# Re-planning an adaLN feed-forward block on one core: new duration tables, smaller transfer margins for the last pair, four PSUM banks for the quarter that TensorE turns

## The chip, the cores and the metric

The kernel runs on one core of one Trainium2 chip. The metric is the device time of that core in microseconds. A run of the kernel before took 563.19 us (median of 3 runs, 563.15 to 563.2).

## The reference

Two conditioning rows select shift, scale and gate by a matmul (adaLN); `x` is 2 x 2048 tokens of 512 features, all in float32.

```
emb = silu(t) @ ada_w + ada_b            # 6 groups of 512
shift_msa, scale_msa, gate_msa, shift_mlp, scale_mlp, gate_mlp = split(emb, 6)
norm = ln(x) * (1 + scale_msa) + shift_msa
h = gelu(norm @ ssm_w1 + ssm_b1);  x = x + gate_msa * (h @ ssm_w2 + ssm_b2)
norm2 = ln(x) * (1 + scale_mlp) + shift_mlp
hf = gelu(norm2 @ ff_w1 + ff_b1)         # 512 -> 1024
x = x + gate_mlp * (hf @ ff_w2 + ff_b2)  # 1024 -> 512
```

## The kernel before

**The work.** The 4096 tokens are eight blocks of 512. Each block is normalized, modulated, turned (features on partitions) and passed through `ssm1` and `ssm2`; then the feed-forward pair follows for four pairs of blocks, `ff1 0`, `ff2 0`, ..., `ff1 3`, `ff2 3`. The four matrix products are done by the Strassen-Winograd scheme, seven products of half-size blocks in place of eight, and in `ff1` and `ff2` the scheme is used twice. TensorE (PE) therefore has fewer matmuls, and VectorE (DVE) and GpSimd (POOL) have hundreds of adds instead: sums of operand blocks that matmuls read, and sums that take products out of PSUM banks. A product lands in one of eight banks, and the next product for that bank waits until the adds have read the last one.

**What sets the order.** Nothing runs when the code calls it. Each helper (`tt` for adds at L258, `act`, `copy`, `mm` at L296, `turn_by_pe` at L306, `dma` at L318) records an operation with a cost, a latency and its dependencies in `Plan`. The PE operations keep the order of the code. `Plan.order` works back from the PE operations to a due time for every other operation; `Plan.simulate` then plays the engines forward, and on each takes the most urgent of the operations that could start by its reckoning. An add whose operands lie in SBUF may go to DVE or POOL, whichever reaches it first. The resulting order is what each engine's queue holds, and on the chip a queue runs strictly in that order: an instruction that waits holds all behind it. Costs and latencies are written into the helpers as numbers. DMAs are reckoned with a `care` that stretches them, so that the operations ahead of them are due earlier.

**The start.** PE does nine 512-wide matmuls and one transpose of 48 rows of conditioning data into bank 1 (L306); DVE copies them out (`cols`, L1318). Meanwhile DVE computes mean and variance of the first four token tiles (`BN_STATS` L526, `BN_AGGR` L527; tiles 0 and 1 in `marks_128`, 2 and 3 in `marks_129`), POOL takes the power -0.5 (L559, L560), DVE refines it (L562 to L565) and scales tile 0 (L585), ACT scales tile 1 (L276). PE then makes `modulation` 0 and 1 (L296, 128x128), turns tiles 0 and 1 by eight transposes between the two halves of modulation 1, and tiles 2 and 3 by eight behind it; DVE and ACT take them out (L660, L276), and `ssm1` begins.

**The end.** Of the output of the last pair (`ff2 3`), quarters are turned back by a DVE transpose (L1073, in `quarter_out`) and a trip through DRAM (`back<-far`, then `rows<-back`), and added to the residual (`far<-rows`, `near<-rows`, L258), which is sent out. The last quarter is turned by PE instead (`turned_by_pe`): two transposes of 128x128 per piece into a PSUM bank, a DVE add of that bank to the residual (`hidden<-bank`, 128x2x128), and a DMA of 128 KB. `TURNED_AT` gives the bank: for block 0 of the pair 3 and 4, for block 1 of the pair 2 and 0, one bank for each half, so the two pieces of a half (`e` 0 and 1) share it. `L1049` is the scaled add that takes a finished product out of PSUM into `rows`.

In the listings of orders and in the profile, `rows`, `hidden`, `near`, `far`, `turned`, `ring`, `fw` are SBUF regions; `bank_72` to `bank_79` are PSUM banks 0 to 7.

Of the kernel before, what the change touches and what calls it, by code (L numbers as in the profile page):

```python
# [12 lines left out]
ALU = mybir.AluOpType  # L13
# [7 lines left out]
class Plan:  # L21
# [8 lines left out]
    ISSUE, FLIGHT, LANDING, RATE, BACKLOG = 640.0, 1300.0, 700.0, 370.0, 4000.0  # L30
    NEAR, SPARE = 30000.0, 1500.0
    RATED, LANDED = 0.5, 4000.0
    LITTLE = 1 << 15
    LANES = 8
    AHEAD, SLACK = 2500.0, 150.0

# [76 lines left out]
    def simulate(self):  # L113
        ops, hop = self.ops, self.HOP
        left, ready = [len(op.deps) for op in ops], [0.0] * len(ops)
        free = dict.fromkeys("pvags", 0.0)
        self.lock, pipe, holder = 0.0, 0.0, None
        tensor = [op for op in ops if op.engs == "p"]
        at, pools, found = 0, {e: [] for e in "vags"}, {}
        lanes = [0.0] * self.LANES  # L120

        def enter(op):
            if op.lead and op.late < 1e8:
                ready[op.n] = max(ready[op.n], op.late - op.lead)
            for e in op.engs:
                if e != "p":
                    pools[e].append(op)
                    found.pop(e, None)

        def choose(e):  # L130
            pool = pools[e]
            if not pool:
                return None
            at = {}
            for op in pool:
                backlog = self.BACKLOG if op.late < free[e] + self.NEAR else self.SPARE
                wait = self.lock if e in op.shared else pipe - backlog if op.size > self.LITTLE else 0.0
                at[op.n] = max(free[e], ready[op.n], wait, lanes[0] if op.size else 0.0)
            now = min(at.values())

            def rank(op):
                return op.late + (self.AHEAD if e == "v" and len(op.engs) > 1 else 0.0), op.n

            op = min((op for op in pool if at[op.n] <= now), key=rank)
            end = now + op.cost[e]
            soon = [u for u in pool if now < at[u.n] < end - self.SLACK and u.late < min(end, op.late)]
            if soon:
                op = min(soon, key=lambda u: (at[u.n], u.n))
            return at[op.n], op

        for op in ops:
            if not op.deps:
                enter(op)
        count = len(ops)
        while count:
            best = None
            if at < len(tensor) and not left[tensor[at].n]:
                best = (max(free["p"], ready[tensor[at].n]), -1.0, "p", tensor[at])
            for e in "avgs":
                if e not in found:  # L160
                    found[e] = choose(e)
                c = found[e]
                if c and (best is None or (c[0], c[1].late) < best[:2]):
                    best = (c[0], c[1].late, e, c[1])
            start, _, e, op = best
            op.on, op.start, op.after = e, start, None
            free_at, free[e] = free[e], start + op.cost[e]
            if op.size > self.LITTLE:
                pipe = max(start + self.FLIGHT, pipe) + op.size / self.RATE * (1 + self.RATED * op.care)
                op.end = pipe + self.LANDING + self.LANDED * op.care  # L170
                found.pop("a", None), found.pop("s", None)
            else:
                op.end = start + op.lat[e]
                if op.size and e == "s":
                    op.end = max(op.end, pipe + self.LANDING)
            if op.size:
                lanes = lanes[1:] + [op.end]
                found.pop("a", None), found.pop("s", None)
            if e in op.shared:
                if e == "g" and holder and holder.on == "v" and start > max(free_at, ready[op.n]):  # L180
                    op.after = holder
                self.lock, holder = start + op.cost[e], op
                found.clear()
            if e == "p":
                at += 1
            else:
                for x in op.engs:
                    pools[x].remove(op)
                    found.pop(x, None)
            count -= 1  # L190
            for s in op.succ:
                o = ops[s]
                gap = 0.0 if o.engs == e and not op.size else hop
                ready[s] = max(ready[s], op.end + gap)
                left[s] -= 1
                if not left[s] and o.engs != "p":
                    enter(o)
# [3 lines left out]
def kernel(  # L201
# [62 lines left out]
        )  # L264

    def small(e, fn, o, ins, cost=None):
        cost = cost or {"v": 110, "g": 210}[e]
        plan.add(e, fn, [o], ins, {e: cost}, {e: cost + 75}, "g")

    def act(o, a, func, bias=0.0, scale=1.0):  # L270
        n = cols(o)
        ptrs = [p for p in (bias, scale) if not isinstance(p, float)]
        cost = n / 1.4 + (155, 215, 340)[len(ptrs)] + (30 if func == AF.Gelu_apprx_tanh else 0)
        plan.add(
            "a",
            lambda E: E.activation(o, a, func, bias=bias, scale=scale),  # L276
            [o],
            [a] + ptrs,
            {"a": cost},
            {"a": cost + 90},  # L280
        )

    def copy(o, a):
        cost = cols(o) / 1.4 + 150
        plan.add("a", lambda E: E.copy(o, a), [o], [a], {"a": cost}, {"a": cost + 60})  # L285

    def mm(o, lhsT, rhs, start, stop, at=None):
        n = cols(rhs)
        if at is None:
            cost = {128: 223.0, 256: 431.6, 512: 853.0}.get(n, 2 * (n / 1.2 + 3))  # L290
            kw = {}
        else:
            cost, kw = 68.0, {"tile_position": at}
        plan.add(
            "p",
            lambda E: E.matmul(o, lhsT, rhs, start=start, stop=stop, skip_group_check=True, **kw),  # L296
            [o],
            [lhsT, rhs],
            {"p": cost},
            {"p": cost + 165},  # L300
        )
# [218 lines left out]
    def stats(xt, slots=range(C)):  # L520
        t = marks[norms[0] % 4]
        norms[0] += 1
        mv = cut(t[:, :8], "p (c two) -> p c two", c=C)
        for c in slots:
            st, src, dst = t[:, 8 + 6 * c : 14 + 6 * c], xt[:, c, :], mv[:, c, :]
            plan.add("v", lambda E, st=st, src=src: E.bn_stats(st, src), [st], [src], {"v": 694}, {"v": 680})  # L526
            plan.add("v", lambda E, st=st, dst=dst: E.bn_aggr(dst, st), [dst], [st], {"v": 100}, {"v": 182})  # L527
        return t, mv

    STATS_BY_ACT = (4, 5)  # L530

    def act_sum(o, a, func, total, bias, scale):
        ptrs = [] if isinstance(bias, float) else [bias]
        cost = cols(o) / 1.4 + (440, 540)[len(ptrs)]
        plan.add(
            "a",
            lambda E: E.activation(o, a, func, bias=bias, scale=scale, accum_out=total),
            [o, total],
            [a] + ptrs,
            {"a": cost},  # L540
            {"a": cost + 90},
        )
# [12 lines left out]
    def scales(t, mv, v="g", slots=slice(0, C)):  # L555
# [1 line left out]
        ve, r, e, rstd, nmr = [a[:, slots] for a in full]  # L557
        var, mean, half = mv[:, slots, 1], mv[:, slots, 0], half_t[:, slots]
        small("g", lambda E: E.tensor_scalar(ve, var, 1.0, EPS, ALU.mult, ALU.add), ve, [var])  # L559
        small("g", lambda E: E.tensor_tensor(r, ve, half, ALU.pow), r, [ve, half], 1090)  # L560
        if v == "v":
            small(v, lambda E: E.tensor_tensor(e, r, ve, ALU.mult), e, [r, ve])  # L562
            small(v, lambda E: E.scalar_tensor_tensor(e, e, -0.5, r, ALU.mult, ALU.mult), e, [e, r])
# [28 lines left out]
    def turn(bl, src, c):  # L592
        o = cut(bl, "p (m k c q) -> p k m c q", m=C, k=KD, c=C)[:, :, :, c, :]
        a = cut(slot(src, c), "p (k m q) -> p k m q", k=KD, m=C)
        plan.add("v", lambda E: E.transpose(o, a), [o], [a], {"v": 636}, {"v": 705})

    def modulate(t, k, which, b):
        o = t[:, :, k * P : (k + 1) * P]
# [466 lines left out]
    def quarter_out(s, d, blk, r, scaled=False):  # L1065
# [4 lines left out]
        band = cut(bands[n], "p (a c e r) -> p e c a r", a=M, c=C, e=2)  # L1070
        for e in range(2):
            o, a = band[:, e], cut(done[:, e], "p (c a q) -> p c a q", c=C, a=M)
            plan.add("v", lambda E, o=o, a=a: E.transpose(o, a), [o], [a], {"v": 636}, {"v": 705})  # L1073
        closing = s + 1 == NBLK // 2
        queue = lambda f: "sa"[f % 2] if closing else "s"
        far_t = back_d[s][d][blk]
        for f in range(M):
# [16 lines left out]
        if not closing:  # L1094
            dma(to, x)
        quarters[0] += 1

    def down(s):
        q = {f"{o + 1}{blk + 1}": hC[:, blk, :, 2 * o : 2 * o + 2, :] for o in range(2) for blk in range(2)}
# [81 lines left out]

        return sums, last_sum, prepare, leaf

    TURNED_AT = ((3, 4), (2, 0))
    tail, waiting, leaves_read = [{}, {}], [], [0]

    def turned_by_pe(blk, r, f, quad):
# [3 lines left out]

        def turned_back():
            e, h = int(quad[0]) - 1, int(quad[1]) - 1
            bank = cut(banks[TURNED_AT[blk][h]], "p (c e d) -> p c e d", c=2, e=2)
            for c in range(2):
                col = slice((2 * h + c) * P, (2 * h + c + 1) * P)
                turn_by_pe(bank[:, c, e], summed[:, r, e, col], ident, c == 0 and h not in got, c == 1)
            got[h] = True
            c, d = slice(2 * h, 2 * h + 2), slice(e * P, (e + 1) * P)
            x = got["x"][:, c, d]  # L1200
# [250 lines left out]
```

## Time and profile before

| | |
|---|---|
| median of the runs | 563.19 us |
| profiled execution, its time | 563.11 us |
| span of its trace | 561.3 us |
| mean granted TensorE clock | 0.998 |
| PE busy | 552.9 us (98%), 2809 matmul records |
| DVE busy | 479.2 us (85%), 848 instructions |
| POOL busy | 385.0 us (69%), 475 |
| ACT busy | 282.9 us (50%), 523 |
| DMA | 123.68 MB, mean 220 GB/s |

The profiled execution's own time is 1.8 us above the span, which runs from the first to the last record. PE records overlap, so where time is lost on PE is read from the distance between starts: a 128x256 record begins 0.216 us after the one before it when nothing holds it, a group of four 0.86 us after the last four.

### The profile page before, as it was taken

What the parts mean: (1) busy time and instruction counts of PE and PEld (TensorE: products, weight loads), DVE (VectorE), ACT (ScalarE), POOL (GpSimd) and SP (SyncE); (2) the same over time, 40 slices, a digit from 0 to 9 for tenths busy, and PEclk for the clock granted to TensorE, in tenths of its full rate; (3) what the DMA queues carried; (4) which work ended last, traced back from release to release, by engine and by line L of the source; (5) the groups of instructions that cost most, each with busy time, mean ns of one, the idle gap of its engine ahead of it and who ended that gap; (6) DMA issues with size and microseconds to landing.
All of it is one profiled execution on the core that took longest, in us unless ns stands there. A gap on an engine that the chain in (4) does not pass through costs nothing.

```text
span 561.3 us, 8747 instructions
## 1 busy us (share of the span) xinstructions
PE 552.9 (98%) x2809; PEld 481.7 (86%) x2809; DVE 479.2 (85%) x848; ACT 282.9 (50%) x523; POOL 385.0 (69%) x475
## 2 busy tenths in 40 slices
PE   8999999999999999999999999999999999999995
PEld 4888889888898988888888888888888888888884
DVE  5696888888779578899999997789988989998987
ACT  3473866674877844666205347414247414244230
POOL 2887747979946299985646868676767766547581
PEclk9999999999999999999999999999999999999999
DMA  8963799988399978995201999611998612983417
GB/s 313 398 229 82 233 363 309 316 259 269 106 276 327 291 311 249 330 292 171 57 20 38 286 322 301 226 39 45 303 325 286 212 39 67 312 288 122 140 45 218
DMA packets 66945, 123.68 MB, mean 220 GB/s; under 512 B 5668, under 2 KB 34260, under 8 KB 65364
## 3 DMA queue, kind: packets, MB, share of 16 engines
q1 hardware_dynamic: 64080, 121.27, 65.9%
q10 hardware_dynamic: 2820, 1.86, 1.3%
q8 instruction: 22, 0.36, 0.3%
q14 instruction: 23, 0.19, 0.1%
HBM read 77.89 MB, written 44.18 MB: 217 GB/s over the span
## 4 chain that ended last, share of the span: by engine, by line
PE 91%; DVE 6%; DMA 2%; POOL 0%; issue 0%; DVEq 0%; POOLq 0%
PE bank L296 90%; DVE rows L258 2%; DVE near L258 1%; DMA fw<-in_L_cond_ada_w_dram 1%; DVE far L258 1%; PE bank L306 1%; DVE fw L258 1%; DVE hidden L258 0%; DMA fw<-in_L_cond_ada_b_dram 0%; DVE far L1073 0%; POOL far L258 0%; POOL fw L258 0%; POOL rows L258 0%; DVE turned L660 0%; DVE rows L1049 0%
## 5 line engine op out<-in xcount | busy, mean ns | idle before, releaser
L296 PE MATMUL bank<-turned,ring 128*128 128x256 f32 x896 | 210.2, 380 | 0.2 <-DVE turned L660 0.2
L296 PEld LDWEIGHTS bank<-turned,ring 128*128 128x128 f32 x896 | 168.0, 190 | 23.1 <-DVE turned L660 0.4
L258 DVE TENSOR_TENSOR hidden<-bank,hidden 128x512 f32<-128x512 f32 (+2 forms) x178 | 126.4, 738 | 23.9 <-PE bank L296 19.9
L296 PE MATMUL bank<-near,hidden 128*128 128x256 f32 (+1 forms) x470 | 95.1, 350 | 0.0
L296 PEld LDWEIGHTS bank<-near,hidden 128*128 128x128 f32 x470 | 82.2, 191 | 9.3 <-POOL near L258 0.3
L296 PE MATMUL bank<-far,fw 128*128 128x256 f32 (+1 forms) x354 | 86.0, 374 | 0.2
L258 POOL TENSOR_TENSOR turned<-turned 128x512 f32<-128x512 f32 (+1 forms) x62 | 70.4, 1148 | 20.4 <-DVE turned L258 9.0
L296 PE MATMUL bank<-ring 128*128 128x256 f32 x336 | 82.4, 380 | 0.0
L258 DVE TENSOR_TENSOR rows<-bank,rows 128x256 f32<-128x256 f32 (+1 forms) x142 | 66.1, 478 | 16.0 <-PE bank L296 11.9
L296 PEld LDWEIGHTS bank<-far,fw 128*128 128x128 f32 x354 | 66.5, 190 | 9.6 <-issue 0.5
L296 PEld LDWEIGHTS bank<-ring 128*128 128x128 f32 x336 | 63.7, 190 | 9.0 <-issue 0.5
L285 ACT COPY bank<-bank 128x512 f32<-128x512 f32 (+2 forms) x84 | 37.7, 449 | 63.0 <-PE bank L296 62.2
L276 ACT ACTIVATE hidden<-hidden,cols 128x512 f32<-128x512 f32 (+1 forms) x66 | 44.7, 710 | 42.9 <-DVE hidden L258 42.9
L258 POOL TENSOR_TENSOR hidden<-hidden 128x128 f32<-128x128 f32 (+2 forms) x45 | 43.5, 976 | 25.3 <-DVE hidden L258 13.1
L296 PE MATMUL bank<-near,fw 128*128 128x256 f32 (+1 forms) x246 | 60.7, 377 | 0.0
L296 PE MATMUL bank<-hidden,fw 128*128 128x256 f32 (+1 forms) x216 | 53.3, 376 | 0.4 <-DVE rows L258 0.4
L296 PEld LDWEIGHTS bank<-near,fw 128*128 128x128 f32 x246 | 46.1, 190 | 6.4 <-issue 0.2
L276 ACT ACTIVATE turned<-turned,mod,mod 128x512 f32<-128x512 f32 x56 | 42.2, 807 | 9.0 <-DMA turned<-turned 8.4
L296 PEld LDWEIGHTS bank<-hidden,fw 128*128 128x128 f32 x216 | 40.3, 190 | 6.5 <-DVE rows L258 0.8
L258 POOL TENSOR_TENSOR ring<-turned,ring 128x256 f32<-128x256 f32 x42 | 30.6, 740 | 20.7 <-PE bank L296 17.0
L276 ACT ACTIVATE rows<-rows,gb,mod 128x512 f32<-128x512 f32 (+1 forms) x34 | 26.5, 787 | 34.9 <-DVE rows L258 25.0
L258 POOL TENSOR_TENSOR fw<-fw 128x256 f32<-128x256 f32 (+1 forms) x38 | 35.6, 944 | 11.8 <-DMA fw_parts<-fw 4.3
(123 smaller groups left out, 735.7 us busy)
## 6 DMA issues: line engine op xcount, KB each, us to landing
ring<-fw_parts SPq DMA_DIRECT2D x28, 512.0 KB, 4.8
turned<-far SPq DMA_DIRECT2D x52, 256.0 KB, 4.2
ring<-fw_parts SPq DMA_DIRECT2D x28, 384.0 KB, 5.2
turned<-turned SPq DMA_DIRECT2D x32, 256.0 KB, 5.4
back<-far SPq DMA_DIRECT2D x52, 128.0 KB, 2.9
rows<-back SPq DMA_DIRECT2D x13, 512.0 KB, 5.1
fw_parts<-fw SPq DMA_DIRECT2D x21, 256.0 KB, 4.6
fw<-in_L_cond_ada_w_dram SPq DMA_DIRECT2D x5, 1024.0 KB
```

Source lines behind the costliest of these rows:

```text
L258: lambda E: E.tensor_tensor(o, a, b, f),
L276: lambda E: E.activation(o, a, func, bias=bias, scale=scale),
L285: plan.add("a", lambda E: E.copy(o, a), [o], [a], {"a": cost}, {"a": cost + 60})
L296: lambda E: E.matmul(o, lhsT, rhs, start=start, stop=stop, skip_group_check=True, **kw),
L306: lambda E: E.matmul(o, a, identity, start=start, stop=stop, is_transpose=True, skip_group_check=True),
```

## The change

It changes numbers, and one table. In `Plan` the engines start at 700 ns instead of 0, and large DMAs at 2650. The cost and latency of several kinds of operations are replaced: small POOL and DVE operations, narrow ACT operations, copies, accumulating ACT operations, the modulation matmuls, `BN_STATS` (694 to 585), `BN_AGGR`, the power, the DVE transposes. In `quarter_out` the DMAs of the last pair are recorded with `care` 0.1. `TURNED_AT` gets a bank for every piece, so that block 0 uses banks 3, 0, 2 and 4 for its four pieces.

```diff
-    LITTLE = 1 << 15
+    LITTLE, FIRST = 1 << 15, 2650.0
...
-        free = dict.fromkeys("pvags", 0.0)
-        self.lock, pipe, holder = 0.0, 0.0, None
+        free = dict.fromkeys("pvags", 700.0)
+        self.lock, pipe, holder = 0.0, self.FIRST, None
...
-            plan.add("v", lambda E, st=st, src=src: E.bn_stats(st, src), [st], [src], {"v": 694}, {"v": 680})
-            plan.add("v", lambda E, st=st, dst=dst: E.bn_aggr(dst, st), [dst], [st], {"v": 100}, {"v": 182})
+            plan.add("v", lambda E, st=st, src=src: E.bn_stats(st, src), [st], [src], {"v": 585}, {"v": 680})
+            plan.add("v", lambda E, st=st, dst=dst: E.bn_aggr(dst, st), [dst], [st], {"v": 90}, {"v": 178})
...
         closing = s + 1 == NBLK // 2
+        care, plan.care = plan.care, 0.1 if closing else plan.care
...
         quarters[0] += 1
+        plan.care = care
...
-    TURNED_AT = ((3, 4), (2, 0))
+    TURNED_AT = (((3, 0), (2, 4)), ((2, 2), (0, 0)))
...
-            bank = cut(banks[TURNED_AT[blk][h]], "p (c e d) -> p c e d", c=2, e=2)
+            bank = cut(banks[TURNED_AT[blk][h][e]], "p (c e d) -> p c e d", c=2, e=2)
...
-                turn_by_pe(bank[:, c, e], summed[:, r, e, col], ident, c == 0 and h not in got, c == 1)
+                turn_by_pe(bank[:, c, e], summed[:, r, e, col], ident, c == 0 and (not blk or h not in got), c == 1)
```

PE's order stays the same up to the last six transposes. On DVE and POOL nearly the whole queue is permuted: 93 adds that DVE did are POOL's now, and 88 of POOL's are DVE's (DVE 848 instructions before and 845 now, POOL's adds 416 and 419). Three places are shown; two lines more in the file shift the line numbers from L1106 on by two (L1318 becomes L1320, L1328 becomes L1330).

**The start, DVE.** DVE's queue from its first `BN_STATS` to the first scaled tile's chain, before; `cols<-bank_73` is the copy of PE's 48-row transpose.

```order
L526 BN_STATS marks_128<-far 128x6
L527 BN_AGGR marks_128<-marks_128 128x2
L526 BN_STATS marks_128<-far 128x6
L526 BN_STATS marks_129<-far 128x6
L527 BN_AGGR marks_128<-marks_128 128x2
L527 BN_AGGR marks_129<-marks_129 128x2
L1318 COPY cols<-bank_73 128x48
L526 BN_STATS marks_129<-far 128x6
L527 BN_AGGR marks_129<-marks_129 128x2
L1328 TENSOR_SCALAR cols<-cols 128x4 x2
L562 TENSOR_TENSOR marks_128<-marks_128 128x2
```

The same stretch in the changed kernel:

```order
L526 BN_STATS marks_128<-far 128x6
L1320 COPY cols<-bank_73 128x48
L527 BN_AGGR marks_128<-marks_128 128x2
L1330 TENSOR_SCALAR cols<-cols 128x4
L526 BN_STATS marks_128<-far 128x6
L526 BN_STATS marks_129<-far 128x6
L527 BN_AGGR marks_128<-marks_128 128x2
L1330 TENSOR_SCALAR cols<-cols 128x4
L527 BN_AGGR marks_129<-marks_129 128x2
L526 BN_STATS marks_129<-far 128x6
L527 BN_AGGR marks_129<-marks_129 128x2
L562 TENSOR_TENSOR marks_128<-marks_128 128x2
```

The copy stood behind three `BN_STATS` and three `BN_AGGR`; now it stands behind one `BN_STATS`, and all the others are behind it.

**The first `ff2`, DVE.** DVE's queue in `ff2 0`, about 288.6 to 293.8 us of the trace before; the `fw<-fw` adds prepare operand sums of the second feed-forward weight for the next matmuls, `rows<-bank` and `rows<-rows` empty banks.

```order
L258 TENSOR_TENSOR rows<-rows 128x256
L258 TENSOR_TENSOR rows<-bank_74,rows 128x2x256
L258 TENSOR_TENSOR rows<-bank_73,rows 128x256
L258 TENSOR_TENSOR rows<-rows 128x256
L258 TENSOR_TENSOR fw_71<-fw_71 128x256
L258 TENSOR_TENSOR rows<-bank_76,rows 128x2x256
L258 TENSOR_TENSOR far<-near,far 128x512
L258 TENSOR_TENSOR rows<-bank_74,rows 128x2x256
L258 TENSOR_TENSOR far<-hidden,far 128x512
```

And now:

```order
L258 TENSOR_TENSOR rows<-rows 128x256 x2
L258 TENSOR_TENSOR rows<-bank_74,rows 128x2x256
L258 TENSOR_TENSOR rows<-bank_76,rows 128x2x256
L258 TENSOR_TENSOR rows<-bank_73,rows 128x256
L258 TENSOR_TENSOR fw_71<-fw_71 128x256
L258 TENSOR_TENSOR far<-hidden,far 128x512
L258 TENSOR_TENSOR near<-near 128x2x256
L258 TENSOR_TENSOR rows<-bank_74,rows 128x2x256
```

The two `fw<-fw` are not the same add. The one before stands now some 30 DVE instructions earlier, ahead of the first adds of `ff2 0` that empty banks; the one now is the add that POOL did at 292.54 in the trace before. `far<-near,far` is POOL's now, `near<-near` was POOL's.

A second place of the same kind, told here in words: in `ff2 2` the `rows<-rows` of 128x256 that POOL did at 459.47 stands now on DVE, right behind the `rows<-bank_79` whose result it takes and right ahead of the `rows<-bank_74` (128x512) that takes its own; the `rows<-bank_76` (128x512) and the `far<-hidden,far` that DVE did ahead of them stand behind them.

**The end, DVE.** The last rows of DVE's queue before, from the scaled add of bank 7 on; `hidden<-bank` takes a turned piece, `near<-rows` needs the trip through DRAM.

```order
L1049 SCALAR_TENSOR_TENSOR rows<-bank_79,mod_125,rows 128x256
L258 TENSOR_TENSOR hidden<-bank_75,hidden 128x2x128
L1049 SCALAR_TENSOR_TENSOR rows<-bank_73,mod_125,rows 128x256
L258 TENSOR_TENSOR hidden<-bank_76,hidden 128x2x128 x2
L258 TENSOR_TENSOR hidden<-bank_75,hidden 128x2x128
L258 TENSOR_TENSOR near<-rows,near 128x512 x2
```

The same rows now:

```order
L1049 SCALAR_TENSOR_TENSOR rows<-bank_79,mod_125,rows 128x256
L258 TENSOR_TENSOR hidden<-bank_75,hidden 128x2x128
L258 TENSOR_TENSOR near<-rows,near 128x512 x2
L1049 SCALAR_TENSOR_TENSOR rows<-bank_73,mod_125,rows 128x256
L258 TENSOR_TENSOR hidden<-bank_76,hidden 128x2x128
L258 TENSOR_TENSOR hidden<-bank_74,hidden 128x2x128
L258 TENSOR_TENSOR hidden<-bank_72,hidden 128x2x128
```

The two `near<-rows` stood last and stand now ahead of the last scaled add; the three last pieces lie in three banks (4, 2, 0) where two of them shared bank 4 and one was in bank 3. PE's last six transposes go to banks 4, 2 and 0, two each, where four went to bank 4 and two to bank 3.

More of the change, by code (lines that the diff above doesn't have):

```diff
@@ L266, in small @@
     def small(e, fn, o, ins, cost=None):
-        cost = cost or {"v": 110, "g": 210}[e]
-        plan.add(e, fn, [o], ins, {e: cost}, {e: cost + 75}, "g")
+        cost = cost or {"v": 110, "g": 168}[e]
+        plan.add(e, fn, [o], ins, {e: cost}, {e: cost + {"v": 60, "g": 32}[e]}, "g")
     def act(o, a, func, bias=0.0, scale=1.0):
@@ L272, in act @@
         ptrs = [p for p in (bias, scale) if not isinstance(p, float)]
[L273 removed]
+        cost = n / 1.4 + ((155, 215, 340) if n > 256 else (130, 175, 270))[len(ptrs)] + (30 if func == AF.Gelu_apprx_tanh else 0)
         plan.add(
@@ L283, in copy @@
     def copy(o, a):
-        cost = cols(o) / 1.4 + 150
+        cost = cols(o) / 1.2 + 75
         plan.add("a", lambda E: E.copy(o, a), [o], [a], {"a": cost}, {"a": cost + 60})
@@ L292, in mm @@
         else:
-            cost, kw = 68.0, {"tile_position": at}
+            cost, kw = 53.0, {"tile_position": at}
         plan.add(
@@ L533, in act_sum @@
         ptrs = [] if isinstance(bias, float) else [bias]
-        cost = cols(o) / 1.4 + (440, 540)[len(ptrs)]
+        cost = cols(o) / 1.4 + (270, 430)[len(ptrs)]
         plan.add(
@@ L559, in scales @@
         small("g", lambda E: E.tensor_scalar(ve, var, 1.0, EPS, ALU.mult, ALU.add), ve, [var])
-        small("g", lambda E: E.tensor_tensor(r, ve, half, ALU.pow), r, [ve, half], 1090)
+        small("g", lambda E: E.tensor_tensor(r, ve, half, ALU.pow), r, [ve, half], 1015)
         if v == "v":
@@ L594, in turn @@
         a = cut(slot(src, c), "p (k m q) -> p k m q", k=KD, m=C)
-        plan.add("v", lambda E: E.transpose(o, a), [o], [a], {"v": 636}, {"v": 705})
+        plan.add("v", lambda E: E.transpose(o, a), [o], [a], {"v": 618}, {"v": 700})
     def modulate(t, k, which, b):
@@ L1072, in quarter_out @@
             o, a = band[:, e], cut(done[:, e], "p (c a q) -> p c a q", c=C, a=M)
-            plan.add("v", lambda E, o=o, a=a: E.transpose(o, a), [o], [a], {"v": 636}, {"v": 705})
+            plan.add("v", lambda E, o=o, a=a: E.transpose(o, a), [o], [a], {"v": 618}, {"v": 700})
         closing = s + 1 == NBLK // 2
+        care, plan.care = plan.care, 0.1 if closing else plan.care
         queue = lambda f: "sa"[f % 2] if closing else "s"
```

## The prediction

> **What bounds the kernel now.** I read the page's busy shares first, then the waits of PE, then busy time by stretch.
>
> ```profile
> PE 552.9 (98%) x2809; PEld 481.7 (86%) x2809; DVE 479.2 (85%) x848; ACT 282.9 (50%) x523; POOL 385.0 (69%) x475
> ...
> PE bank L296 <- POOL small L323: 1.3, 1, 1.3
> PE bank L306 <- DVE hidden L258: 0.7, 1, 0.7
> PE bank L296 <- DVE rows L258: 0.4, 1, 0.4
> ...
> 240.00:320.00 80.00, 79.74 (x368) 69.29 (x367) 78.20 (x123) 33.91 (x58) 52.68 (x53) 1.00 0.44 137
> 430.00:540.00 110.00, 109.60 (x508) 96.03 (x507) 100.78 (x152) 43.08 (x79) 69.03 (x57) 1.00 0.53 170
> ```
>
> PE is the bound (98% busy). Its matmuls and their order do not change up to the last six transposes. So the change can only win what PE loses to waits: a head of 14 us until `ssm1` runs without a break, a few short stalls in the middle, and a tail of 6.6 us behind PE's main work. Of its waits the 1.3 us for POOL comes before the first matmul and is not touched. The last two rows (busy us of PE, PEld, DVE, ACT, POOL) show where the middle is tight: from 240 to 320 DVE is busy 78.2 of 80 us. There an add that is badly placed becomes a PE stall.
>
> I go through head, middle and tail and sum against the profiled execution, 563.11 us (span 561.3 plus 1.8), which lies 0.08 under the median.
>
> **Head: 1.2 us lost.**
>
> ```profile
> 4.71 0.69 DVE L526 BATCH_NORM_STATS2 marks<-far 128x6 f32<-128x512 f32 x1 [2.77 <-DMA far<-in_x_dram]
> ...
> 6.98 0.30 DVE L527 BATCH_NORM_AGGREGATE marks<-marks 128x2 f32<-128x6 f32 x2
> 7.91 0.21 DVE L1318 COPY cols<-bank 128x48 f32<-128x48 f32 x1 [0.63 <-PE bank L306]
> 8.03 0.68 DVE L526 BATCH_NORM_STATS2 marks<-far 128x6 f32<-128x512 f32 x1
> 8.96 0.15 DVE L562 TENSOR_TENSOR marks<-marks 128x2 f32<-128x2 f32 x1
> ...
> 9.74 0.55 DVE L585 TENSOR_SCALAR far<-far,marks 128x512 f32<-128x512 f32 x1
> 7.50 0.73 POOL L560 TENSOR_TENSOR marks<-marks,small 128x2 f32<-128x2 f32 x1
> 9.85 0.80 ACT L276 ACTIVATE far<-far,marks 128x512 f32<-128x512 f32 x1
> 7.64 0.23 PE L306 MATMUL bank<-far,fw 48*128 48x48 f32 x1 [0.21 <-DMA fw<-in_L_cond_ff_b_dram]
> 11.10 1.09 PE L306 MATMUL bank<-far 128*128 128x128 f32 x8
> 12.12 0.65 PE L296 MATMUL bank<-fw,far 128*32 128x128 f32 x16
> 14.00 0.92 PE L296 MATMUL bank<-turned,ring 128*128 128x256 f32 x3 [0.21 <-DVE turned L660]
> ```
>
> The copy `cols` cannot start before PE's 48-row transpose, which starts at 7.64 because a DMA lands then. It ran at 7.91, and DVE had done three `BN_STATS` by then. In the new order one `BN_STATS` is ahead of it, so DVE, done at 5.40, idles 2.5 us. Behind the copy (next start 8.03) come `BN_AGGR` and one `TENSOR_SCALAR` (about 0.1 us each), tile 1's `BN_STATS` at 8.24, tile 2's 0.6 later, tile 1's `BN_AGGR` at 9.46, ended 9.64. It ended at about 7.16 before. POOL's power took 1.07 us from the end of that `BN_AGGR` to its own end (8.23), so it ends at 10.71. DVE's chain L562 to L565, 0.78 us from start to start of what follows it (8.96 to 9.74 before), starts there, since `BN_STATS` no longer delays it: L585 at 11.54 instead of 9.74, 1.8 later; ACT's tile at 11.65, done 12.45.
>
> PE turns tile 0 first, so its second transpose waits for ACT's tile: 12.49 instead of some 11.27. The seven left and the next matmul follow as before (12.12 less 11.27 is 0.85): modulation 1 goes on at 13.34, not 12.12, and `ssm1` starts at 15.2, not 14.00. Tiles 2 and 3 are done at 13.6 and 13.8 by the same steps, just ahead of PE's 13.9, so no more is added; that is a margin of 0.1 and I bound the loss by 0.9 and 1.7. Behind 14 us PE has almost no idle time, so nothing swallows this.
>
> **Middle: 1.3 us won, bounds 2.1 won and 1.0 lost.**
>
> ```profile
> 288.96 1.03 PE L296 MATMUL bank<-near,fw 128*128 128x256 f32 x4
> 290.01 1.10 PE L296 MATMUL bank<-hidden,fw 128*128 128x256 f32 x4
> 291.25 1.10 PE L296 MATMUL bank<-far,fw 128*128 128x256 f32 x4
> 292.19 1.03 PE L296 MATMUL bank<-hidden,fw 128*128 128x256 f32 x4
> 293.32 0.92 PE L296 MATMUL bank<-far,fw 128*128 128x256 f32 x3
> 290.11 0.65 DVE L258 TENSOR_TENSOR rows<-rows 128x256 f32<-128x256 f32 x1
> 290.69 0.41 DVE L258 TENSOR_TENSOR fw<-fw 128x256 f32<-128x256 f32 x1
> 289.21 1.27 POOL L258 TENSOR_TENSOR far<-near 128x512 f32<-128x512 f32 x1 [2.36 <-DVE rows L258]
> 292.54 0.73 POOL L258 TENSOR_TENSOR fw<-fw 128x256 f32<-128x256 f32 x1 [0.63 <-DVE far L258]
> ...
> 459.47 0.72 POOL L258 TENSOR_TENSOR rows<-rows 128x256 f32<-128x256 f32 x1
> 460.23 1.02 DVE L258 TENSOR_TENSOR rows<-bank,rows 128x512 f32<-128x512 f32 x2 [1.22 <-POOL rows L258]
> 459.55 1.03 PE L296 MATMUL bank<-near,fw 128*128 128x256 f32 x4
> 460.98 1.13 PE L296 MATMUL bank<-hidden,fw 128*128 128x256 f32 x4 [0.40 <-DVE rows L258]
> ```
>
> Sixteen records from 288.96 to 293.32 took 4.36 us, at 0.216 each they take 3.46: **0.9 lost**, to the `fw<-fw` that DVE ended at 291.10 and the one that POOL ended at 293.26 (PE goes on 0.15 and 0.06 behind them), and to a DVE that was late with its banks. The first now stands before the adds of `ff2 0`, and the second moves to DVE ahead of `far<-hidden,far`. By the rows' durations DVE reaches it at about 291.1 and ends it at 291.5, before PE comes for it. I take 0.7 of the 0.9.
>
> At 460, `rows<-rows` waited on POOL behind another add, and DVE, which idled 1.22 us for it, emptied bank 2 only then: PE's four started 0.57 and more late (459.55 to 460.98 is 1.43, 0.86 is usual). Now DVE does that add right behind its producer, 0.4 us instead of 0.72 and nothing ahead of it: **0.6 won**. Shorter waits elsewhere are left out: 0.7 + 0.6 = 1.3.
>
> The gain is bounded at 2.1: both places whole (1.5), and for the shorter waits, which I did not add up, once more the 0.6 of the second place. The bound of 1.0 lost is three stalls like those above (0.46 and 0.57) in place of what goes: 181 adds change engine, and POOL's take longer (0.73 for 256 columns against 0.41), some 10 us more POOL work in all.
>
> A row bears on that. `rows<-rows` at 290.11 took 0.65 where `fw<-fw` of the same size took 0.41, and it ended at 290.76, 0.28 after POOL's add ended (290.48): DVE stood still for POOL. The Trainium skill states this in "SBUF — State Buffer", section "Who interferes with whom": a DVE operation with two SBUF inputs and a GpSimd one that reads SBUF share a port pair that is locked for a whole instruction, the other blocks. The trace agrees here. By that rule 10 us more of POOL are up to 10 us more in which such an add stands still, and the sum would move towards that of the third rival below, 564.9, instead of 561.9.
>
> **Tail: 1.4 us won, bounds 1.7 won and 0.6 lost.**
>
> ```profile
> 554.83 0.48 DVE L1049 SCALAR_TENSOR_TENSOR rows<-bank,mod,rows 128x256 f32<-128x256 f32 x1 [0.24 <-PE bank L296]
> 555.23 0.41 DVE L258 TENSOR_TENSOR hidden<-bank,hidden 128x256 f32<-128x256 f32 x1
> 555.70 0.66 PE L306 MATMUL bank<-far,rows 128*128 128x128 f32 x4 [0.69 <-DVE hidden L258]
> ...
> 556.85 1.28 DVE L258 TENSOR_TENSOR near<-rows,near 128x512 f32<-128x512 f32 x2
> 558.16 0.38 ACTq L318 DMA_DIRECT2D out_dram<-near  x1
> 550.98 0.53 SPq L318 DMA_DIRECT2D rows<-back  x1
> 551.59 0.60 ACTq L318 DMA_DIRECT2D rows<-back  x1
> out_dram<-hidden ACTq DMA_DIRECT2D x4, 128.0 KB, 2.7
> ```
>
> PE's last four transposes waited 0.69 us for the add that reads bank 4, then the last pieces and two `near<-rows` followed, and the last DMA (256 KB) went out at 558.16, 3.1 before the span's end. Now the bank is another and that wait goes; the two `near<-rows` (1.28) move ahead of the last scaled add. From the end of bank 3's piece, about 554.5: `near` to 555.75, scaled add to 556.2, the piece in bank 4 (turned long before) to 556.5, bank 2 to 556.85, bank 0 to 557.2. PE turns the last two pairs in 0.7 from 556.2 on, so they are there in time. The last DMA goes out at 557.25, and it is a 128 KB one, 2.7 us by the last row: the end is at 559.9, not 561.3. `out<-near`, issued at 555.8 at the latest, ends sooner.
>
> The price of putting `near<-rows` first: it needs `rows<-back`. The SP one was issued at 550.98, which I leave; ACT's stands now ahead of `out<-far` and comes perhaps 1 us sooner than 551.59. Their packets took to about 554.5 and 555.3. A landing later than 554.5 holds DVE and PE's last transposes one for one. The gain is used up at 555.9.
>
> **Sum.** 563.11 + 1.2 - 1.3 - 1.4 = 561.6. I add 0.3 for the SP half landing a little late, as its rows leave no margin at all: 561.9.
>
> **The rivals.**
> 1. *The middle gives nothing*: new stalls replace the old. For it: DVE 98% busy from 240 to 320. Against: both places named are mended in the order. 563.11 + 1.2 - 1.4, and half a us of the late half: 563.2, no change.
> 2. *The trip through DRAM is late*, and DVE, which waits in `near<-rows`, holds the last scaled add. It decides from a landing at 554.5 on; at 556.0 it costs 1.5: 561.6 + 1.5 = 563.1. For it: DVE's transposes of that quarter stand behind two more scaled adds (0.7 each). Against: ACT issues its half earlier.
> 3. *POOL is late (slower)*: it holds the port pair for 10 us more, an add that PE waits for comes late in `ff2` where DVE has 2 to 9 us free in 80 to 110. Four pairs, a stall of 0.5 in each and none of the old ones gone: 563.11 + 1.2 + 2.0 - 1.4 = 564.9. With the old stalls left in place the kernel is slower from 1.4 us of new ones on, three of them. Against: the new order gives DVE less work.
> 4. *The head loses nothing*, because the DMA behind the 48-row transpose lands 2 us sooner: 560.4. The rows before speak against it, nothing about that DMA changes.
>
> **How the numbers follow.** The forecast 0.52, rival 1 0.18, rival 2 0.12, rival 3 0.14, rival 4 0.04. A measurement of this kernel tells about 0.2%, 1.1 us, from no change: faster is below 562.06, slower above 564.3. The forecast's own spread (560.9 to 562.9) lies about two thirds on the faster side: 0.35, with rival 4 and a little of rival 2 faster 0.42. Slower is rival 3 and a little of the rest, 0.15, the same 0.43. The range goes from 560.4, the middle at its bound or the head unharmed, to 564.5, part of rival 3.
>
> **What would show it.** Head: `cols` stands second on DVE, 2 us idle before it, and `ssm1` starts near 15.2. Middle: no PE gap at `ff2 0` and `ff2 2` where `fw<-fw` and `rows<-rows` were waited for. Tail: PE waits for no `hidden`, DVE ends on a piece, `near<-rows` shows no idle ahead of it by a DMA, and the span ends some 2.7 behind the last issue. Wrong would make it above all a new group of PE waits for POOL or DVE `L258`, or `rows<-back` as the releaser of DVE in the last 8 us.

## The result, and the profile after

The changed kernel took 566.64 us (median of 6 runs, 566.15 to 567.16) against 563.21 (563.15 to 563.29): ratio 1.0061, interval 1.0048 to 1.0074. It is slower by 3.4 us where 1.3 less was forecast, and above the range. Its runs also scatter by 1 us, the six of before beside them by 0.14. The profiled execution took 566.70, span 564.9. Its page and its waits of PE:

```profile
PE 553.4 (98%) x2809; PEld 481.6 (85%) x2809; DVE 480.2 (85%) x845; ACT 280.4 (50%) x523; POOL 396.5 (70%) x478
...
PE bank L306 <- DVE rows L1049: 2.9, 1, 2.9
PE bank L296 <- POOL small L323: 1.3, 1, 1.3
PE bank L296 <- DMA ring<-fw_parts: 1.1, 1, 1.1
PE bank L306 <- DVE far L585: 1.1, 1, 1.1
PE bank L296 <- DVE rows L1049: 0.4, 1, 0.4
PE bank L296 <- DVE hidden L258: 0.3, 1, 0.3
```

The shares of busy time say nothing: PE is 98% busy in both. The waits say most: 0.7 and 0.4 us of before are gone, and five new ones of 0.3 to 2.9 us stand there. Both traces have 2809 PE records in one order (only the banks of the last six transposes differ), so the start of the n-th can be laid beside the start of the n-th; where the difference jumps, time was lost or won:

```
                                     before    after    jump
third transpose of the start          11.38    12.64   +1.27
ssm, near 121 and 145                144.78   146.63   +0.58
a ring load, near 229                229.39   232.62   +1.38
ff2 0, 290 to 293                    293.32   295.72   -0.82
ff1 1, near 320                      321.52   324.16   +0.24
ff2 2, 460                           460.98   463.09   -0.53
ff2 3, near 552                      551.53   554.20   +0.55
the shared bank, 555.7               555.70   557.52   -0.85
the last two transposes              555.98   560.77   +2.98
from there to the end of the span      5.32     4.13   -1.19
sum                                                    +3.6
```

**The start** came as forecast. DVE (first four rows), ACT and PE of the changed kernel:

```profile
4.93 0.69 DVE L526 BATCH_NORM_STATS2 marks<-far 128x6 f32<-128x512 f32 x1 [2.99 <-DMA far<-in_x_dram]
8.03 0.21 DVE L1320 COPY cols<-bank 128x48 f32<-128x48 f32 x1 [2.40 <-PE bank L306]
8.35 1.28 DVE L526 BATCH_NORM_STATS2 marks<-far 128x6 f32<-128x512 f32 x2
11.61 0.55 DVE L585 TENSOR_SCALAR far<-far,marks 128x512 f32<-128x512 f32 x1
...
11.61 0.81 ACT L276 ACTIVATE far<-far,marks 128x512 f32<-128x512 f32 x1 [1.55 <-DVE marks L565]
...
12.22 1.25 PE L306 MATMUL bank<-far 128*128 128x128 f32 x8 [1.05 <-DVE far L585]
15.27 0.92 PE L296 MATMUL bank<-turned,ring 128*128 128x256 f32 x3 [0.21 <-DVE turned L660]
```

DVE stands idle 2.40 us ahead of the copy; L585 starts at 11.61 (11.54 was worked out), `ssm1` at 15.27 (15.2).

**The two mended places** of the middle, PE at 290 and at 460 of before:

```profile
292.27 1.03 PE L296 MATMUL bank<-near,fw 128*128 128x256 f32 x4
293.13 1.03 PE L296 MATMUL bank<-hidden,fw 128*128 128x256 f32 x4
294.00 1.03 PE L296 MATMUL bank<-far,fw 128*128 128x256 f32 x4
...
462.23 1.03 PE L296 MATMUL bank<-near,fw 128*128 128x256 f32 x4
463.09 1.03 PE L296 MATMUL bank<-hidden,fw 128*128 128x256 f32 x4
```

Groups of four follow each other after 0.86 or 0.87 us: no wait is left at either place.

**The tail** went the other way. The last rows of DVE, the chain that ended last over the same stretch, and PE's last transposes:

```profile
556.82 0.41 DVE L258 TENSOR_TENSOR hidden<-bank,hidden 128x256 f32<-128x256 f32 x1
559.01 1.31 DVE L258 TENSOR_TENSOR near<-rows,near 128x512 f32<-128x512 f32 x2 [1.78 <-DMA rows<-back]
560.24 0.48 DVE L1049 SCALAR_TENSOR_TENSOR rows<-bank,mod,rows 128x256 f32<-128x256 f32 x1
560.63 1.07 DVE L258 TENSOR_TENSOR hidden<-bank,hidden 128x256 f32<-128x256 f32 x3
...
549.66 3.61 DMA back<-far
553.29 5.63 DMA rows<-back
...
560.77 0.44 PE L306 MATMUL bank<-far,rows 128*128 128x128 f32 x2 [2.87 <-DVE rows L1049]
```

DVE idles 1.78 us in `near<-rows` for `rows<-back`, and behind it the last scaled add and PE's last transposes wait. That is the second rival, and dearer than it was priced (1.5 us for a landing at 556.0).

### The profile page after: what moved, and what is told of

The parts are those of the page before. It is cut to its first block, busy times and chain, and to the rows that moved or that the text cites. A ratio compares the mean times of both kernels' runs of the same rounds, so it can differ in the third digit from the quotient of the medians.

```text
span 564.9 us, 8741 instructions
## 1 busy us (share of the span) xinstructions
PE 553.4 (98%) x2809; PEld 481.6 (85%) x2809; DVE 480.2 (85%) x845; ACT 280.4 (50%) x523; POOL 396.5 (70%) x478
## 4 chain that ended last, share of the span: by engine, by line
PE 80%; DVE 11%; POOL 3%; DMA 3%; issue 2%; ACT 1%; DVEq 0%; ACTq 0%; POOLq 0%
PE bank L296 79%; DVE rows L258 3%; DVE hidden L258 2%; DMA ring<-fw_parts 1%; DVE turned L258 1%; DMA rows<-back 1%; DVE rows L1049 1%; DVE far L258 1%; DVE far L1073 1%; POOL turned L258 1%; DVE far L595 1%; DVE near L258 1%; DMA back<-far 1%; DVE marks L526 1%; POOL hidden L258 0%
## 5 line engine op out<-in xcount | busy, mean ns | idle before, releaser
L258 POOL TENSOR_TENSOR turned<-turned 128x512 f32<-128x512 f32 (+1 forms) x57 | 63.3, 1126 | 13.0 <-DVE turned L258 6.5
L276 ACT ACTIVATE hidden<-hidden,cols 128x512 f32<-128x512 f32 (+1 forms) x66 | 44.8, 710 | 43.8 <-DVE hidden L258 43.6
L258 POOL TENSOR_TENSOR hidden<-hidden 128x128 f32<-128x128 f32 (+2 forms) x47 | 48.8, 1048 | 24.3 <-DVE turned L258 7.1
L276 ACT ACTIVATE turned<-turned,mod,mod 128x512 f32<-128x512 f32 x56 | 42.0, 805 | 8.4 <-DMA turned<-turned 8.0
L258 POOL TENSOR_TENSOR ring<-turned,ring 128x256 f32<-128x256 f32 x41 | 29.6, 731 | 19.6 <-PE bank L296 15.2
L258 POOL TENSOR_TENSOR fw<-fw 128x256 f32<-128x256 f32 (+1 forms) x39 | 33.1, 856 | 11.7 <-DVE fw L258 3.6
L276 ACT ACTIVATE rows<-rows,gb,mod 128x512 f32<-128x512 f32 (+1 forms) x34 | 25.8, 784 | 24.7 <-DVE rows L258 23.4
```

Source lines behind the costliest of these rows:

```text
L258: lambda E: E.tensor_tensor(o, a, b, f),
```

## The experiments

The change falls into four parts that can be undone one by one. The starting times move only the first 12 rows of DVE, the margin only the last 37 rows of DVE (in the changed kernel from 541 us on, where three adds also change places between DVE and POOL) and a few DMAs, the banks five rows of DVE and PE's last six transposes; all the rest of the new order comes from the table of durations.

### e1 to e4: one part undone, or one part alone

e1 takes the margin out of the changed kernel:

```diff
-        care, plan.care = plan.care, 0.1 if closing else plan.care
...
-        plan.care = care
```

> The changed kernel with the old margin (0.45) on the last pair's transfers; the orders differ only in the last 35 rows of DVE and a few of ACT and SP, and both near<-rows stand last again, behind the turned pieces. Theory (the small margin let the plan put near<-rows ahead of the last scaled add, where it waits for rows<-back): PE's wait of 2.9 us before its last two transposes goes, near<-rows ends the program again some 2.8 us after the last scaled add, 565.3 us (565.0 to 565.7), 1.3 less than the 566.6 of the changed kernel. Rival (the trip through DRAM itself is late, because the transposes ahead of it moved): DVE waits for rows<-back at the end as long as before, 566.4 to 566.8.

566.7 us (565.49 to 567.5), ratio 1.0064 (1.0048 to 1.0081): by the median the rival. The trace says that the theory held for the tail and the middle hid it: DVE no longer waits for `rows<-back`, PE's last two transposes lost 0.3 instead of 2.98, and from 541 us on, where the orders part, e1 is 1.0 us quicker. But PE was already 0.8 us later there than in the changed kernel, with the same order up to that place. The orders with the new table do not run alike each time.

e2 puts the four banks alone into the kernel before (the `TURNED_AT` lines of the diff).

> The kernel before with the four banks alone; only the last six transposes and five DVE rows differ, near<-rows stays last. Theory (the shared bank made PE wait 0.69 us and all behind it is in line): near<-rows ends 0.35 us sooner, since the last scaled add at 555.31 now bounds PE; 562.85 us (562.6 to 563.0). Rival (the end is set by transfers): no change, 563.2.

562.72 us (562.46 to 563.14), ratio 0.9995 (0.9985 to 1.0004). PE no longer waits for `hidden` at the end, its last transposes come 0.72 sooner, 0.6 of it won there. The 0.3 us against the runs beside it (563.02) fits the theory but is inside the interval.

e3 puts the margin alone into the kernel before.

> The kernel before with the small margin alone (0.1); one near<-rows now stands ahead of the piece in bank 4 and the other ahead of the last scaled add, all before 550 us as it was. Theory (the place of near<-rows costs): DVE waits for rows<-back, the last scaled add and the last transposes wait behind it, 564.5 us (563.8 to 565.3). Rival (the margin only moves the issues earlier and the landing is in time): 562.5 to 563.2.

562.95 us (562.73 to 564.17), ratio 1.0002 (0.9993 to 1.0011): no loss, against the theory. Its DVE waits only 0.7 us for `rows<-back`. The last DMAs are of 128 KB and came as late as before (issue at 558.22, 558.16 in the kernel before).

e4 gives the changed kernel the old starting times.

```diff
-    LITTLE, FIRST = 1 << 15, 2650.0
+    LITTLE, FIRST = 1 << 15, 0.0
...
-        free = dict.fromkeys("pvags", 700.0)
+        free = dict.fromkeys("pvags", 0.0)
```

> The changed kernel with the old starting times of the plan (engines 0, transfers 0); only the first 12 rows of DVE differ, the copy stands behind three BN_STATS again. Theory: ssm1 starts at 14.0 instead of 15.27 and all else stays, 565.4 us (565.1 to 565.7). Rival (the later waits are for transfers, whose times hang on the loads and not on PE, so they grow by what the head wins): 566.6.

565.92 us (565.16 to 566.47), ratio 1.0051 (1.0036 to 1.0066): 0.7 less than the changed kernel, between theory and rival. In its trace PE starts `ssm1` at 14.10 and is level with before, within 0.1, up to 82 us, so the head is back whole; then it meets 1.1 us near 318 and 1.2 near 412, more than the changed kernel's own profile had.

### e5 to e8: the table, and single moves by hand

e5 has the old starting times and the old margin; what is left is the table, and the banks.

> The changed kernel with both the old starting times and the old margin: what is left of the change is the table of durations (and the four banks). The middle has the changed kernel's order. Theory: head as before, the waits at 290 and 460 us of before gone (1.4 won), new stalls near 121 and 145 (0.6), 318 (1.1) and at a ring load (1.2), a late scaled add near 550 (0.5), banks 0.3 won: 565.0 us (564.4 to 565.8). Rival (the tables are harmless, the loss came with start and margin): 562.0 to 563.0.

564.4 us (563.72 to 564.7), ratio 1.0018 (1.0009 to 1.0028). Table and banks together cost 1.2 us, net of the gains at 290 and 460. Against e4 the old margin is worth 1.5 us. For e6 to e8 the emitted order is edited by hand behind the planner, nothing else changes on any engine:

```diff
-    for op in plan.order():
+    queue = plan.order()
...
+    for n, m in ((1670, 1832), (2580, 2837)):   # e6; e7: ((2392, 2298),); e8: all three
+        later(n, m)                              # op n is emitted right behind op m
+    for op in queue:
```

> As e5, and on SP alone two stores moved behind the two ring loads that followed them: one x store near 223 us and one out store near 407 us. Theory (SP's queue is in order, a store that waits for its add holds the load behind it, and PE waits for the load): the stall of 1.2 us at a ring load goes, 563.8 us (563.2 to 564.4). Rival (the transfers are late because the 16 DMA engines are full there): no change against e5.

564.37 us (563.64 to 564.91), ratio 1.0018 (1.0008 to 1.0027): as e5. It tells nothing, since in e5's trace PE does not wait for a ring load at all.

> As e5, and on DVE alone one add with two SBUF inputs (far<-hidden, near 317 us) moved behind the seven adds that follow it, six of which empty banks. Theory (that add stands still for 1.07 us while POOL's near<-rows runs, and the adds that PE waits for stand behind it): the stall near 318 of 1.0 us goes, 564.0 us (563.4 to 564.7). Rival (DVE is simply late there): no change against e5.

563.12 us (562.64 to 564.02), ratio 0.9999 (0.9989 to 1.0008): 1.3 less than e5, all from one add in another place. DVE and POOL of e5 near 318, and PE:

```profile
317.92 1.75 DVE L258 TENSOR_TENSOR far<-hidden 128x512 f32<-128x512 f32 x1
319.60 1.47 DVE L258 TENSOR_TENSOR hidden<-bank,hidden 128x512 f32<-128x512 f32 x2
...
317.66 1.46 POOL L258 TENSOR_TENSOR near<-rows,near 128x512 f32<-128x512 f32 x1
...
318.33 1.03 PE L296 MATMUL bank<-ring 128*128 128x256 f32 x4
320.33 1.13 PE L296 MATMUL bank<-ring 128*128 128x256 f32 x4 [0.98 <-DVE hidden L258]
```

And of e7:

```profile
318.59 2.70 DVE L258 TENSOR_TENSOR hidden<-bank,hidden 128x512 f32<-128x512 f32 x4
321.21 0.74 DVE L258 TENSOR_TENSOR far<-hidden 128x512 f32<-128x512 f32 x1
...
318.75 1.28 POOL L258 TENSOR_TENSOR near<-rows,near 128x512 f32<-128x512 f32 x1 [0.68 <-DVE ring L258]
...
317.29 1.89 PE L296 MATMUL bank<-ring 128*128 128x256 f32 x8
319.02 2.75 PE L296 MATMUL bank<-turned,ring 128*128 128x256 f32 x12
```

In e5 `far<-hidden`, two inputs from SBUF, takes 1.75 us: POOL's add runs to 319.12, and 0.55 later DVE's is done. PE waits for the `hidden<-bank` behind it. In the kernel before, this add stood in the same place on DVE; there POOL was idle and did `near<-rows` only at 324:

```profile
316.86 0.68 DVE L258 TENSOR_TENSOR far<-hidden 128x512 f32<-128x512 f32 x1
317.62 1.27 POOL L258 TENSOR_TENSOR far<-rows,far 128x512 f32<-128x512 f32 x1 [0.96 <-DVE far L258]
324.10 2.52 POOL L258 TENSOR_TENSOR near<-rows,near 128x512 f32<-128x512 f32 x2 [1.23 <-DVE far L258]
```

In e7 four adds that read PSUM run at 0.68 or 0.69 each beside POOL's adds, undisturbed, `far<-hidden` takes 0.74, and PE runs through.

> Both moves of e6 and e7 on top of e5. Theory (two separate stalls): both gains add, 562.9 us (562.2 to 563.6). Rival (when one stall goes the next late transfer or add is met sooner): gains add to less than 1.2, above 563.8.

563.2 us (562.95 to 563.63), ratio 0.9999 (0.9989 to 1.0008). The gains do not add, as e6 had none to give. Table and banks with this one add moved are as fast as the kernel before.

### e9 to e12: the gains without the losses

e9: margin and banks together in the kernel before.

> The kernel before with the small margin and the four banks, old table and old start. Theory (the forecast of the tail was right where rows<-back is issued near 551 as it was, and failed in the changed kernel since it is issued 2.3 us later there): near<-rows waits some 0.7 us for its transfer, the last issue is a 128 KB one, 562.2 us (561.9 to 562.6), 0.5 under the banks alone. Rival (near<-rows ahead of the last scaled add costs in any order): 562.7 to 563.6.

563.21 us (562.82 to 564.05), ratio 1.0001 (0.9991 to 1.001): the rival. The last rows of DVE in e9:

```profile
554.34 0.42 DVE L258 TENSOR_TENSOR hidden<-bank,hidden 128x256 f32<-128x256 f32 x1
555.95 1.29 DVE L258 TENSOR_TENSOR near<-rows,near 128x512 f32<-128x512 f32 x2 [1.20 <-DMA rows<-back]
557.16 0.48 DVE L1049 SCALAR_TENSOR_TENSOR rows<-bank,mod,rows 128x256 f32<-128x256 f32 x1
557.56 1.09 DVE L258 TENSOR_TENSOR hidden<-bank,hidden 128x256 f32<-128x256 f32 x3
```

Here both halves of `rows<-back` were issued at 551.25, about as in the kernel before, and the add still waited to 555.95, 4.7 us. So the tail's forecast fails in the old order too, and a late issue is not the reason there.

e10: banks in the kernel before, and by hand only what mends 290 and 460.

```diff
+    # 460: POOL's rows<-rows to DVE behind its producer, rows<-bank_76 and far<-hidden behind rows<-bank_74
+    # 290: DVE's fw<-fw to POOL ahead of its add at 285.59; POOL's next fw<-fw one place ahead
+    for move in ((3032, "behind", 3031, "v"), (3028, "behind", 3035), (3018, "behind", 3028),
+                 (1338, "ahead", 2073, "g"), (1339, "ahead", 1337)):
+        place(*move)
```

> The kernel before with the four banks and, by hand, only those moves of the new order that end PE's waits: at 460 POOL's rows<-rows on DVE behind its producer, the adds of bank 4 and far<-hidden behind it; at 290 one fw<-fw from DVE to an idle place of POOL near 284 us and POOL's other fw<-fw one place ahead. Theory (the middle's gain of the new order is these waits and can be had alone): 0.5 won at 460 and 0.5 at 290, 561.7 us (561.4 to 562.1). Rival (what is taken from one place is late in the next, as in the new order): 562.4 to 563.0.

562.8 us (562.72 to 562.94), ratio 0.9991 (0.9982 to 1.0001): 0.44 under the runs beside it, hardly more than the 0.30 that the banks gave alone. In its trace 460 gives 0.4, but at 290 PE is 0.6 later first, and still 0.5 later at 459, by this chain (DVE, then POOL, then PE):

```profile
283.76 1.21 DVE L258 TENSOR_TENSOR far<-near,far 128x512 f32<-128x512 f32 x1
...
283.52 0.90 POOL L258 TENSOR_TENSOR fw<-fw 128x256 f32<-128x256 f32 x1
...
289.00 1.03 PE L296 MATMUL bank<-near,fw 128*128 128x256 f32 x4
290.61 1.10 PE L296 MATMUL bank<-hidden,fw 128*128 128x256 f32 x4 [0.58 <-DVE rows L258]
```

The add given to an idle POOL held up DVE's `far<-near,far` by 0.53 (it took 0.68 before, at 283.70), and DVE, full from there on, brought that to PE.

> e9 and e10 together. Theory (middle and tail are separate): gains add, 561.2 us (560.8 to 561.6). Rival (the trip through DRAM does not come earlier when PE does): no better than e10, 561.7 or more.

563.28 us (563.1 to 564.44), ratio 1.0 (0.999 to 1.0009): the rival. In its trace PE waits 1.9 us ahead of its last two transposes.

e12: e5 with `HOP` 150 instead of 70.

> As e5 (new table, old start, old margin, four banks), and the plan's allowance from engine to engine is 150 ns instead of 70, so every step is due 80 ns earlier. Theory (the new table leaves the plan too little slack, and adds fall into POOL's adds): fewer of the small stalls, 563.2 us (562.6 to 563.8). Rival (any new plan shuffles the adds and meets its own few collisions): other stalls at other places, 563.8 to 565.5.

563.29 us (562.95 to 566.48), ratio 1.0011 (0.9995 to 1.0028). The median is the theory's, the trace is the rival's: the stall at 318 is gone, a new one of 1.4 us for ACT's `turned` (L276) stands near 82, with others near 208 and 214. Two of its ten runs took 566.5. It does not tell them apart.

### e13 to e16: the changed kernel again

> The changed kernel once more, beside the next three on the same chip: 566.6 us (566.1 to 567.2).

566.56 us (566.42 to 567.72), ratio 1.0064 (1.0049 to 1.0079). Its trace has no wait for a ring load, but 1.1 at 318, and the same 3.0 at the end. So the stall at 229 is no standing cost: without it PE loses, counted as in the table of jumps, 1.0 near 318 instead of 0.24, and the time is the same.

> The changed kernel with e6's two moves on SP (stores behind the ring loads). Theory (the load waits behind a store in SP's queue): the wait of PE for ring<-fw_parts goes, 1.0 us less than e13, 565.6 us, and less scatter. Rival (full DMA engines): the same as e13, the wait stays in the trace.

566.91 us (565.77 to 567.43), ratio 1.0063 (1.0048 to 1.0078): the rival for the time. No wait for a ring load shows in its trace, but neither does one in e13's. The SP order as a standing cause falls; as an occasional one it is only argued.

> The changed kernel with e7's move on DVE alone. In its trace the stall near 318 was 0.5 us, in e4 and e5 1.1. Theory (the add stands still behind POOL's): 0.5 to 1.1 less than e13, 565.8 us (565.3 to 566.2). Rival: the same as e13.

566.0 us (565.0 to 566.7), ratio 1.0048 (1.0033 to 1.0063): 0.56 less than e13, at the low end of the theory, on four runs each whose ranges overlap. The stall at 318 is gone from its trace.

> The changed kernel with the old margin and the moves of e6 and e7: only the new starting times are left of what costs. Theory (the head's 1.27 us stands alone and is carried to the end): e8's 563.2 and 1.3, 564.5 us (564.1 to 564.9). Rival (a later PE finds its adds and transfers in time and catches up): 563.2 to 563.9.

564.92 us (564.05 to 565.74), ratio 1.0028 (1.0019 to 1.0038): 1.7 more than e8: the theory, 0.4 dearer than worked out. Against e15, which has the new margin (and lacks e6's moves on SP), it is 1.1 less. PE of e16:

```profile
12.56 1.25 PE L306 MATMUL bank<-far 128*128 128x128 f32 x8 [1.35 <-DVE far L585]
13.73 0.65 PE L296 MATMUL bank<-fw,far 128*32 128x128 f32 x16
```

Its wait is the changed kernel's wait; nothing behind it makes it up.

## Why the prediction was wrong, point by point

- **Head, 1.2 lost: right.** The trace has 1.27, e16 against e8 1.7 and e4 against the changed kernel 0.7, on runs that scatter by 0.7 to 1.7. The order of DVE's first rows, with the copy second, is the cause, since e4 moves nothing else.
- **Middle, 1.3 won: the gain was right, the sum was not.** 290 and 460 gave 0.82 and 0.53, 1.35 together. The step that failed is "Shorter waits elsewhere are left out": I looked at the places where PE waits now and not at those where the new order would make it wait. These took back 2.2 us in the changed kernel's profile. The stalls near 121 and 145 (0.6 together) and one near 552 (0.4 to 0.6, counted with the tail below) stand in every trace with the table except e12's; what sets them was not tried. The largest that returned in most traces (changed kernel, e1, e4, e5, e6, e13, e14) is `far<-hidden` behind POOL's `near<-rows` near 318, 1.3 us by e5 against e7. That is the third rival's mechanism, in `ff1` and not in `ff2` where I had looked for it, and I had priced it at four stalls of 0.5 without looking up the place: the two engines' orders side by side would have shown that `near<-rows` had moved ahead by six us (324.10 before, 317.66 in e5). Of the adds that change engine 92 go to POOL and 89 to DVE, not 93 and 88; the 181 stand.
- **Tail, 1.4 won: wrong, 1.5 lost** (0.55 - 0.85 + 2.98 - 1.19; the 0.55 is the table's stall near 552). The failed step is the trip through DRAM: the prediction took over a landing near 554.5 from the old order, with ACT's half issued perhaps 1 us sooner. Each of the two transfers leaves sixteen semaphore events in the trace, and the last is its landing (558.92 in the changed kernel, where DVE goes on at 559.01). In the kernel before the halves landed at 554.91 and 555.73, 3.9 and 4.15 us behind their issues, so the ends of the packets were 0.4 early, which the 0.3 added to the sum nearly covers. Less the 2.1 us by which all of PE was later, the changed kernel issued ACT's half at 551.2 and SP's at 551.5, each about 0.6 later than forecast, and ACT's half, which DVE's first `near<-rows` takes, landed at 556.8, 2.3 later than 554.5 and 5.6 us behind its issue. Fifteen of its sixteen events had come 2.2 us sooner, at 554.6, where the forecast had it; the last one held DVE. The same late sixteenth (1.9 to 2.2 us) stands in the traces of e4, e13, e14 and e15, all with the new table and the new margin. In the other thirteen traces it is at most 0.3 behind the fifteenth, and both halves land 3.4 to 4.7 us behind their issues. What held it is not shown.
- In e9, without that late event, ACT's half still landed at 555.93, later than before (555.73) though issued 0.3 us sooner: the 1 us for going ahead of `out<-far` did not come. The page of before had a row `rows<-back`, 5.1 us to landing, for whole quarters of 512 KB; 550.98 and 5.1 is 556.1, which would have pointed to the second rival (break-even 555.9), but the halves of that same trace took 3.9 and 4.15. The terms around the trip were right: PE no longer waits for the bank (0.85 won), the last issue is 128 KB and the end comes 1.2 us sooner behind PE's last transposes.
- **The margin's other side.** e9 against the banks alone (0.5 by the medians, 0.3 by the ratios), e4 against e5 (1.5) and e15 against e16 (1.1) agree that the new margin costs, where `near<-rows` stands ahead of the last scaled add. e1 against the changed kernel shows no such gain in the time, only in the trace from 541 on. In e3, where the margin alone cost nothing, a turned piece stands between the two `near<-rows`, and DVE waits 0.7.
- **The sum.** Head 1.3, middle 0.8, tail 1.5 make the 3.6 of the span. Of the rivals, the second and third came together, each given about one chance in eight, and I had not formed the case of both. (The first rival's own terms, with half a us, come to 563.4, not 563.2.)
- **What stays open.** The orders with the new table scatter by 0.7 to 2 us from run to run (e12 by 3.5), the order of before by 0.14 beside the first runs of the changed kernel and by 0.6 to 1.3 over the 13 to 31 runs beside the experiments. Stalls at ring loads near 229 (changed kernel) and 412 (e1, e4), and others near 82 (e1, e5, e16) and 175 (e5, e15), come and go, and e14 did not settle what starts those at the loads. What delays the last sixteenth of `rows<-back` where the new table and the new margin meet was not tried. No version beat the kernel before beyond doubt: the banks alone (562.72, 0.9995) and e10 (562.8, 0.9991) are lowest, both with intervals that reach 1.

## What to carry to other kernels

When an order is planned anew, the waits that vanish are seen in the old trace, and the new ones are not: read the two engines that share a port side by side in the new order, at every place where the filled one feeds PE. A transfer's time in the old order is not its time in the new one (here 3.9 to 4.15 us became 5.6 to 6.0), and it counts to the last of its events: an add that waits for it belongs behind everything that doesn't. That durations "as traced" leave the plan too little slack was not shown: e12, which gave it more, had the theory's median and the rival's trace.

## What the runs showed of the hardware

An add of DVE with two inputs in SBUF stands still while POOL's add runs, in e5 for 1.07 us (1.75 against 0.68 for 128x512), and ends about 0.55 behind POOL's end (e5 and e10); adds with one input in PSUM run beside POOL's adds at 0.68 or 0.69 as ever (e7). The Trainium skill has this in "SBUF — State Buffer", section "Who interferes with whom"; the traces agree. In e10 an add given to an idle POOL, 0.90 us there, cost DVE 0.53. Reading back 256 KB halves from DRAM in packets of 512 bytes, beside two stores of 256 KB, took 3.4 to 4.7 us from issue to landing in thirteen traces and 5.6 to 6.1 in the five where the last of sixteen events came late.
